# Layer b of a hybrid block on one NeuronCore: its block loop written as one sequence, four engines held to it

## The chip, the cores and the metric

The kernel runs on one NeuronCore of a Trainium2 chip. The metric is the time of one execution on the device, in microseconds (us); the time before is the median of three runs. TensorE (PE) multiplies matrices and PEld is its weight loading; VectorE is DVE, ScalarE is ACT, GpSimd is POOL, SyncE is SP.

## The reference

The input `x` has shape (4, 2048, 512). Four residual steps follow each other, each on a layer-normalised copy of `x`:

```python
x = x + _L0_attn_a_ref(_layernorm(x), ...)   # linear attention, 16 heads of 64
x = x + _L0_ffn_ref(_layernorm(x), L0_ffn_rhs)
x = x + _L0_attn_b_ref(_layernorm(x), ...)   # gated recurrence, below
x = x + _L0_ffn_ref(_layernorm(x), L0_ffn_rhs)
```

The feed-forward step quantises each row to 127 levels, multiplies by a quantised 512 x 512 matrix and scales back. Layer b is the third step with the fourth:

```python
q, k, v = x @ q_w.T, x @ k_w.T, x @ v_w.T            # 16 heads of 32
q, k = _apply_rope(q, cos, sin), _apply_rope(k, cos, sin)
q_r, k_r = einsum('bthd,hrd->bthr', q, Wq), einsum(..., k, Wk)   # 16 features a head
g = sigmoid(x @ g_w.T + g_b)
def step(M, inp):
    q_t, k_t, v_t, g_t = inp
    M = M * decay + einsum('bhr,bhd->bhrd', g_t * k_t * scale, v_t)
    return M, einsum('bhr,bhrd->bhd', q_t, M)
out = Y @ out_w.T + out_b
hres = x + out
return layernorm(hres) * ln_g + ln_b
```

## The kernel before, in words

A flag computed from the decays selects the mild variant of both layers; with these inputs it is the one that runs. `layer_a_mild` does the first two steps and stores its rows to `mmid` in DRAM. `layer_b_mild` does the last two. Only the latter is touched.

Layer b walks 32 blocks of 256 rows (4 sequences of 8 blocks). One turn `n` of the loop works on four blocks at once. `B` is block n: the recurrence itself. `after` is block n+1: its projections. `later` is block n+2: its rows are normalised and turned. `before` is block n-1: its second half of the output projection, and its feed-forward step.

The turn has four chunks, c = 0 to 3, for half a block's rows (`i` = c // 2, a row tile of 128) and a group of 8 heads (`g` = c % 2). In each chunk the recurrence is done in matrix form:

- `scores`: TensorE multiplies keys and queries into `ps`, and the carried `state_b` with the queries into `pyT`; VectorE multiplies `ps` by the causal mask into `ab` (two instructions).
- `update`: TensorE makes `pub` from the turned keys `kt` and the values `vb`; VectorE adds it to `pairs`.
- `outputs`: TensorE adds `ab` times `vb` to `pyT` in two halves; ScalarE copies `pyT` to `yT`; GpSimd spreads `pairs` into `state_b`.

Between these stand the projections. `features` multiplies the turned rows `xnTb` by `m_qT` or `m_kT` into `pr` (8 matmuls of the program, 16 passes in the trace, since float32 matmuls appear as two) and VectorE makes the rotary products `xc`, `xs` out of it. `gates` makes `pg`, from which ScalarE makes `gate`; `keys` makes `pl`, from which ScalarE copies `q` and VectorE makes `k`; `values` makes `pvb`, which ScalarE copies to `vb`. `prepare` weighs keys and queries by powers of the decay: `k1` and `qs` on VectorE, four head-masked query copies on ScalarE, `ke` and `q0` on GpSimd. The keys `ke` are turned by a DMA transpose.

The rows: `enter_row` normalises a row tile into `xr` and starts its turning; `turn_row` ends it. Turning means that VectorE splits the float32 words into 16-bit `planes`, SP issues a DMA transpose to `turned`, and ScalarE joins the halves (`turn_halves`, `join_halves`). `turn_row` also adds `ln_b` and `out_b` on GpSimd. `leave` projects `yT` into `py`, adds `xr` into `h`, normalises it, and adds it to `x` on GpSimd. `finish` is the feed-forward step: `ffn_levels` normalises into `f_xn` and rounds into `f_q`, a DMA transpose makes `f_qT`, TensorE makes `pf`, VectorE scales it into `f_y`, GpSimd adds that to `x`.

Every normalisation is a chain over two engines: `bn_stats` and `bn_aggr` on VectorE, two small operations on GpSimd for `rs` (`stats`, lines 124 to 127), then the scaling on VectorE (`normalize`, line 131).

PSUM is in tagged banks: three for `mm` (all projections), two for `s` (`ps`), two for `y` (`pyT`), one for `u` (`pub`). The pools are single or double buffered, so each tag hands its buffers round in the order in which they are asked for.

What sets the order: the text of the loop gives each chunk a list of small steps (`fill`), which `spread` deals out among the chunk's own steps in equal portions. After that a scheduler of the tile layer may move instructions among each other on every engine. On the chip each engine takes its instructions in the order that results.

```python
def spread(work, fill):
    at = 0
    for n, f in enumerate(work):
        f()
        upto = len(fill) * (n + 1) // len(work)
        for g in fill[at:upto]:
            g()
        at = upto
```

Of the kernel before, what the change touches and what calls it, by code (L numbers as in the profile page):

```python
# [46 lines left out]
def hybrid_block_kernel(ctx: ExitStack, tc: tile.TileContext, t: dict, out: bass.AP):  # L47
# [82 lines left out]
    def normalize(dst, src, mv, rs, i):  # L130
        nc.vector.tensor_scalar(
            dst, src, mv[:, i, 0:1], rs[:, i : i + 1], ALU.subtract, ALU.mult
        )
# [502 lines left out]
    def run(steps):  # L636
        for f in steps:
            f()
# [76 lines left out]
    def join_halves(dst, turned):  # L715

        nc.scalar.copy(  # L717
            dst.bitcast(U16).rearrange("p n (t two) -> p n t two", two=2),
            turned.rearrange("p (two n) t -> p n t two", two=2),
        )  # L720
# [350 lines left out]
    def layer_b_mild():  # L1071
        with ExitStack() as es:
# [23 lines left out]
            def row_tiles():  # L1096
                return rowp.tile([P, KC, TB], F32, name="xnTb"), rowp.tile([P, NTB, D], F32, name="xr", bufs=4)
# [72 lines left out]
            def block(n):  # L1170
                B = Block()
                B.n, B.first, B.x = n, at[n][1] == 0, xs.pop(0) if xs else load_x(n)
                B.qk, B.turned, B.prep, B.yT, B.halves = {}, {}, {}, {}, {}
                return B

            def enter_row(B, i):

                if i == 0:
                    blk = at[B.n][1]
                    B.cs = []  # L1180
                    for name in ("cos", "sin2"):
                        c1 = rowp.tile([P, TB], F32, name=f"m_{name}", bufs=3)
                        queue = nc.scalar if B.n < 2 else nc.sync
                        queue.dma_start(c1, t[name][:, blk * TB : (blk + 1) * TB])
                        B.cs.append(c1.unsqueeze(1).to_broadcast([P, 2, TB]))
                    B.xnT, B.xr = first_rows.pop() if first_rows else row_tiles()
                mv, rs = stats(pool, B.x[:, i : i + 1, :], 1)
                normalize(B.xr[:, i, :], B.x[:, i, :], mv, rs, 0)
                if B.n > 1:
                    B.halves[i] = turn_halves(pool, B.xr[:, i, :])  # L1190

            def turn_row(B, i):
                dst = B.xnT[:, :, i * P : (i + 1) * P]
                if B.n > 1:
                    join_halves(dst, B.halves[i])
                else:
                    transpose_rows(bank, dst, B.xr[:, i, :], tag="mm")
                nc.gpsimd.tensor_tensor(B.x[:, i, :], B.x[:, i, :], ln_b, ALU.add)
                nc.gpsimd.tensor_tensor(B.xr[:, i, :], B.xr[:, i, :], out_b, ALU.add)
# [69 lines left out]
            def prepare(B, g):  # L1269


                q, k = B.qk[g]
                A = Block()
                A.k1 = pool.tile([P, NTB, NQ, P], F32, name=f"k1{g}", bufs=1)
                nc.vector.tensor_tensor(
                    A.k1,
                    k.rearrange("p (i s) -> p i s", s=P).unsqueeze(2).to_broadcast([P, NTB, NQ, P]),
                    tk[:, g, :, :].unsqueeze(1).to_broadcast([P, NTB, NQ, P]), ALU.mult,
                )
                qs = pool.tile([P, NTB * NQ, QB], F32, name="qs", bufs=1)  # L1280
                nc.vector.tensor_tensor(
                    qs, q.rearrange("p (j s) -> p j s", s=QB),
                    tq[:, g, :].unsqueeze(1).to_broadcast([P, NTB * NQ, QB]), ALU.mult,
                )
                A.q1 = pool.tile([P, NTB * NQ, 4, QB], F32, name=f"q1{g}", bufs=1)
                for h in range(4):
                    nc.scalar.activation(A.q1[:, :, h, :], qs, AF.Copy, scale=small["head4"][:, h : h + 1])
                A.ke = pool.tile([P, NTB, P], F32, name="ke", bufs=1)
                A.q0 = pool.tile([P, NTB, P], F32, name=f"q0{g}", bufs=1)
                for dst, src, tab in ((A.ke, k, down), (A.q0, q, up)):  # L1290
                    nc.gpsimd.tensor_tensor(
                        dst, src.rearrange("p (i s) -> p i s", s=P),
                        tab[:, g, 1 : P + 1].unsqueeze(1).to_broadcast([P, NTB, P]), ALU.mult,
                    )
                A.halves = turn_halves(pool, A.ke.rearrange("p i s -> p (i s)"))
                B.prep[g] = A

            def chunk(B, i, g):

                C = Block()  # L1300
                st = state[:, g, :]

                def turn():
                    A = B.prep[g]
                    if i == 0:
                        A.kt = pool.tile([P, NTB, P], F32, name=f"kt{g}", bufs=1)
                        join_halves(A.kt, A.halves)

                def scores():

# [57 lines left out]
                        small["diag"].rearrange("p (q c) -> p q c", c=2 * DB), ALU.mult,  # L1368
                    )

                return [turn, scores, lambda: None, lambda: run([update, outputs]), lambda: None]

            def leave(B, i):

                def evict(py):
                    h = pool.tile([P, D], F32, name="h")
                    nc.vector.tensor_tensor(h, py, B.xr[:, i, :], ALU.add)
                    mv, rs = stats(pool, h.unsqueeze(1), 1)
                    normalize(h, h, mv, rs, 0)
                    nc.gpsimd.tensor_tensor(h, h, ln_g, ALU.mult)  # L1380
                    x = B.x[:, i, :]
                    nc.gpsimd.tensor_tensor(x, x, h, ALU.add)  # L1382

                return product(
                    bank, "py", [P, D],
                    [(lambda c=c: B.yT[i][:, c, :], lambda c=c: wo[:, c, :]) for c in range(KC)], evict,
                )

            def finish(B, i):
                mul = ffn_product(pool, bank, B.x[:, i, :], *ffn_levels(pool, B.x[:, i, :]))  # L1390

                def store():
                    b, blk = at[B.n]
                    nc.sync.dma_start(rows(out[b], blk * TB, TB), B.x)

                return mul + ([store] if i == NTB - 1 else [])

# [7 lines left out]

            for n in range(2):
                for i in range(NTB):
                    enter_row(get(n), i)  # L1410
                    turn_row(get(n), i)
            get(2)
            fill_tables()
# [1 line left out]
            for g in range(G):  # L1415
                run(features(first, "q", g) + features(first, "k", g) + gates(first, g) + keys(first, g))
                run(values(first, g))
                prepare(first, g)
            for n in range(len(at) + 1):
                B, after, later = blocks.get(n), blocks.get(n + 1), blocks.get(n + 2)  # L1420
                before = blocks.get(n - 1)
                if B and B.first:
                    nc.gpsimd.memset(state, 0.0)
                    nc.gpsimd.memset(pairs, 0.0)
                for c in range(2 * G):
                    i, g = c // G, c % G
                    head, fill = [], []
                    if after:
                        fill += [
                            lambda: features(after, "q", 0) + features(after, "k", 0),  # L1430
                            lambda: gates(after, 0) + keys(after, 0) + features(after, "q", 1),
                            lambda: values(after, 0) + features(after, "k", 1),
                            lambda: gates(after, 1) + keys(after, 1) + values(after, 1),
                        ][c]()

                    if c == 0 and before:
                        fill += leave(before, 1)
                        before.mul = finish(before, 0)
                    if c == 1 and before:
                        head = before.mul  # L1440
                    if c == 2 and before:
                        before.mul = finish(before, 1)
                    if c == 2 and B:
                        fill += leave(B, 0)
                    if c == 3 and before:
                        head = before.mul
                    if later and c in (1, 2):
                        head = head + [lambda i=c - 1: turn_row(later, i)]
                    if later and c in (0, 1):
                        enter_row(later, c)  # L1450
                    if c == 2:
                        get(n + 3)
                    work = chunk(B, i, g) if B else [lambda: None]
                    spread(work, head + fill)
                    if c == 2 and after:
                        prepare(after, 0)
                    if c == 3 and after:
                        prepare(after, 1)

    flag = mild_decays()  # L1460
    with tc.If(flag) as mild:
# [111 lines left out]
```

## Time and profile before

| | us |
|---|---|
| median of 3 runs (lowest, highest) | 4069.87 (4067.77, 4070.08) |
| the profiled execution: time, span | 4071.76, 4070.0 |
| TensorE busy (share of the span) | 3922.4 (96%) |
| VectorE busy | 2350.3 (58%) |
| GpSimd busy | 1479.3 (36%) |
| ScalarE busy | 888.8 (22%) |
| mean granted TensorE clock | 0.991 |
| first `ps` of layer b's loop | at 2507.36 |
| last turns' drain (after 4014), until the last GpSimd add ends | 50 |

The span runs from the first to the last instruction; the time has a little around it. Layer a takes about the first 2450 us of the span, layer b the rest. Busy times of TensorE are modelled, and an engine that is busy may also be held back by another; a row's mean can hold both undisturbed and stretched instances of the same operation. In a timeline row the columns are the start, the duration, the engine, the line and operation, the tiles, the count, and in brackets the idle time before it with what ended it. In a wait row they are who waited for whom: us in total, times, longest. In a row for a stretch of time they are the stretch, its length, then busy us and count for TensorE, its weight loads, VectorE, ScalarE and GpSimd, the granted clock, the DMA share and GB/s.

### The profile page before, as it was taken

The page shows a single profiled execution, that of the slowest core. Times are in us where ns is not written, and L with a number is a line of the kernel's source. Part 1 is how long each engine was busy: PE and PEld are TensorE (multiplying, and loading weights), DVE is VectorE, ACT ScalarE, POOL GpSimd, SP SyncE. Part 2 cuts the span into 40 slices and gives each one's busy share as a digit, 9 for nine tenths or more (in the row PEclk, how much of TensorE's full clock was granted, in tenths as well). Part 3 has the DMA queues.
Part 4 walks back from the last instruction along what each step waited for, and adds up shares of the span by engine and source line. Part 5 has one row for each costly group of instructions (what it writes and reads, how often), then busy time and mean ns, then how long its engine had stood idle before and what let it go on. Part 6 is the DMA issues. An engine that isn't in the chain of part 4 may idle for free.

```text
span 4070.0 us, 53718 instructions
## 1 busy us (share of the span) xinstructions
PE 3922.4 (96%) x20821; PEld 2125.6 (52%) x20821; DVE 2350.3 (58%) x4556; ACT 888.8 (22%) x1548; POOL 1479.3 (36%) x2527
## 2 busy tenths in 40 slices
PE   8999999999999999999999987999999999999997
PEld 4554554554555555555555544555555555555553
DVE  4455555555555555555555454666666666666665
ACT  1222122221221222222122111222222222222221
POOL 3223323323333323323332223444444444444443
PEclk9999999999999999999999998999999999999998
DMA  4112212212212222221221123121211112211211
GB/s 135 31 41 55 67 36 60 62 38 64 55 41 65 55 53 52 55 64 40 54 66 39 38 63 111 43 51 48 52 47 47 47 47 50 50 48 49 53 32 29
DMA packets 432042, 217.27 MB, mean 53 GB/s; under 512 B 363808, under 2 KB 376992, under 8 KB 431776
## 3 DMA queue, kind: packets, MB, share of 16 engines
q1 hardware_dynamic: 430656, 212.16, 21.2%
q8 instruction: 166, 2.72, 0.3%
q10 hardware_dynamic: 1120, 1.57, 0.1%
q14 instruction: 100, 0.82, 0.1%
HBM read 91.49 MB, written 34.08 MB: 31 GB/s over the span
## 4 chain that ended last, share of the span: by engine, by line
PE 68%; DVE 18%; POOL 10%; issue 2%; DMA 2%; ACT 0%; SPq 0%; POOLq 0%; ACTq 0%; DVEq 0%
PE pk L648 11%; PE pq L648 11%; PE pv L648 11%; PE po L648 10%; PE py L648 5%; PE pr L1223 4%; PE pss L888 3%; PE pn L974 3%; DVE st L124 3%; POOL rs L127 3%; PE pn L968 3%; DVE planes L710 2%; POOL h L1380 2%; POOL xb L1382 2%; PE pu L904 2%
## 5 line engine op out<-in xcount | busy, mean ns | idle before, releaser
L648 PE MATMUL pq<-xnTa,a_Wq 128*128 128x512 f32 x1024 | 492.2, 608 | 0.0
L648 PE MATMUL pk<-xnTa,a_Wk 128*128 128x512 f32 x1024 | 491.0, 604 | 0.0
L648 PE MATMUL pv<-a_Wv,xnTa 128*128 128x512 f32 x1024 | 476.1, 603 | 2.9 <-ACT xnTa L141 2.9
L648 PE MATMUL po<-a_Wo_sb,oT 128*128 128x512 f32 x1024 | 467.1, 601 | 6.7 <-DVE oT L950 6.7
L126 POOL TENSOR_SCALAR rs<-mv 128x1 f32<-128x1 f32 x320 | 71.7, 224 | 767.6 <-DVE mv L125 767.3
L914 POOL TENSOR_TENSOR within<-state,u 64x64 f32<-64x64 f32 x256 | 157.3, 615 | 524.4 <-ACT u L909 514.8
L648 PEld LDWEIGHTS po<-a_Wo_sb,oT 128*128 128x128 f32 x1024 | 189.6, 190 | 234.9 <-issue 222.1
L648 PEld LDWEIGHTS pv<-a_Wv,xnTa 128*128 128x128 f32 x1024 | 188.6, 191 | 234.2 <-issue 225.2
L648 PEld LDWEIGHTS pq<-xnTa,a_Wq 128*128 128x128 f32 x1024 | 181.4, 189 | 193.1 <-issue 182.8
L648 PEld LDWEIGHTS pk<-xnTa,a_Wk 128*128 128x128 f32 x1024 | 184.5, 189 | 180.9 <-issue 158.8
L909 ACT COPY u<-pu 128x256 f32<-128x256 f32 x128 | 47.7, 373 | 1026.3 <-PE pu L904 1015.4
L1223 PE MATMUL pr<-xnTb,m_qT_sb 128*128 128x256 f32 x1024 | 252.2, 390 | 0.0
L1223 PE MATMUL pr<-xnTb,m_kT_sb 128*128 128x256 f32 x1024 | 248.9, 386 | 0.0
L648 PE MATMUL pvb<-b_vT_sb,xnTb 128*128 128x512 f32 x512 | 242.8, 607 | 0.0
L894 DVE TENSOR_TENSOR sm<-pss,causal 128x512 f32<-128x512 f32 x256 | 164.2, 683 | 119.9 <-PE pss L888 119.9
L648 PE MATMUL py<-b_oT_sb,yT 128*128 128x512 f32 x512 | 231.8, 595 | 0.0
L717 ACT COPY kr<-turned 128x1024 uint16<-128x1024 uint16 x120 | 139.3, 1161 | 423.6 <-DMA turned<-planes 423.6
L1223 PEld LDWEIGHTS pr<-xnTb,m_qT_sb 128*128 128x128 f32 x1024 | 187.6, 190 | 57.3 <-issue 21.4
L1223 PEld LDWEIGHTS pr<-xnTb,m_kT_sb 128*128 128x128 f32 x1024 | 189.9, 190 | 48.9 <-issue 20.0
L127 POOL TENSOR_TENSOR rs<-rs,neg_half 128x1 f32<-128x1 f32 x320 | 193.9, 607 | 23.9
L838 DVE TENSOR_TENSOR xa<-po,xa 128x512 f32<-128x512 f32 x64 | 44.1, 689 | 262.6 <-PE po L648 262.6
L914 POOL TENSOR_TENSOR within<-within,u 64x64 f32<-64x64 f32 x512 | 173.6, 339 | 38.4
(158 smaller groups left out, 6300.0 us busy)
## 6 DMA issues: line engine op xcount, KB each, us to landing
wide<-rec SPq DMA_DIRECT2D x124, 256.0 KB, 3.6
mmid<-xa SPq DMA_DIRECT2D x16, 1024.0 KB, 4.3
out<-xb SPq DMA_DIRECT2D x32, 512.0 KB, 2.8
xa<-in_x SPq DMA_DIRECT2D x15, 1024.0 KB, 6.3
xb<-mmid SPq DMA_DIRECT2D x30, 512.0 KB, 3.6
turned<-planes SPq DMA_TRANSPOSE x304, 3.1
m_cos<-in_cos SPq DMA_DIRECT2D x30, 128.0 KB, 2.3
m_sin<-in_sin SPq DMA_DIRECT2D x30, 128.0 KB, 2.4
```

The lines of the kernel that those rows point to most:

```text
L124: nc.vector.bn_stats(st[:, i, :], x[:, i, :])
L127: nc.gpsimd.tensor_tensor(rs, rs, neg_half[:, :n], ALU.pow)
L648: nc.tensor.matmul(held[0], lhs(), rhs(), start=(n == 0), stop=(n == len(pairs) - 1))
L710: nc.vector.tensor_copy(planes, src.bitcast(U16).rearrange("p (n two) -> p two n", two=2))
L717: nc.scalar.copy(dst.bitcast(U16).rearrange("p n (t two) -> p n t two", two=2), turned.rearrange("p (two n) t -> p n t two", two=2),)
L888: nc.tensor.matmul(ps[h][:, i, :], k[r, chunks[i]], q[r, chunks[i]], start=True, stop=True)
L894: nc.vector.tensor_tensor(s, ps[h], causal.unsqueeze(1).to_broadcast([P, NTA, P]), ALU.mult)
L904: nc.tensor.matmul(pu[r, i, :], A.kr[:, i, r], v()[:, i, vh[h]], start=True, stop=True, skip_group_check=True,)
L914: nc.gpsimd.tensor_tensor(A.before[i + 1][r, r], A.before[i][r, r], u[r, i, :], ALU.add)
L968: nc.tensor.matmul(pn[:, i, :], A.before[i], q[:, chunks[i]], start=(i == 0), stop=False, skip_group_check=True,)
L974: nc.tensor.matmul(pn[r, i, :], v()[:, i, vh[h]], A.sm[h][:, i, :], start=False, stop=True, skip_group_check=True,)
L1223: nc.tensor.matmul(pr[:, half, :], wp[name][:, c, lo : lo + P], B.xnT[:, c, :], start=(c == 0), stop=(c == KC - 1),)
```

## The change

Three things are done, all in `layer_b_mild`.

The helpers are cut where their chain leaves an engine for GpSimd or for a DMA: `enter_row` becomes `weigh_row` (statistics) and `norm_row` (scaling and planes); `leave` becomes `project`, `weigh_output` and `norm_output`; `finish` becomes `weigh_ffn`, `levels` and `store`; the turning of keys becomes `turn_keys` and `turned_keys`.

The loop over chunks with `fill` and `spread` is replaced by one written sequence for a turn, `blocks_of(n)`. In it every chunk begins with `scores`, one or more whole projections follow, then `update` and `outputs`, then the rest.

The loop over turns stands in `tc.manual_schedule` for TensorE, VectorE, ScalarE and GpSimd: these keep the order of the text. SP, which issues the DMAs, is not in the list. The prologue and layer a are outside it.

```diff
-            for n in range(len(at) + 1):
+            def blocks_of(n):
                 B, after, later = blocks.get(n), blocks.get(n + 1), blocks.get(n + 2)
                 before = blocks.get(n - 1)
...
-                for c in range(2 * G):
...
-                    work = chunk(B, i, g) if B else [lambda: None]
-                    spread(work, head + fill)
+                chunks[0][0]()
+                if before:
+                    weigh_ffn(before, 0)
+                if after:
+                    run(features(after, "q", 0))
+                chunks[0][1]()
+                if later:
+                    weigh_row(later, 0)
+                if before:
+                    levels(before, 0)
+                if after:
+                    run(features(after, "k", 0))
+                if before:
+                    project(before, 1)
+                if B:
+                    turned_keys(B, 1)
+                chunks[1][0]()
+                if before:
+                    weigh_output(before, 1)
+                if after:
+                    run(gates(after, 0) + keys(after, 0))
+                chunks[1][1]()
+                if before:
+                    run(before.levels[0])
+                if later:
+                    norm_row(later, 0)
+                if before:
+                    norm_output(before, 1)
+                if later:
+                    weigh_row(later, 1)
+                if after:
+                    run(features(after, "q", 1))
+                chunks[2][0]()
+                if after:
+                    prepare(after, 0)
+                if before:
+                    weigh_ffn(before, 1)
+                if later:
+                    turn_row(later, 0)
+                if after:
+                    run(values(after, 0))
+                    turn_keys(after, 0)
+                chunks[2][1]()
+                if later:
+                    norm_row(later, 1)
+                if before:
+                    levels(before, 1)
+                if after:
+                    run(features(after, "k", 1))
+                if B:
+                    project(B, 0)
+                get(n + 3)
+                chunks[3][0]()
+                if B:
+                    weigh_output(B, 0)
+                if after:
+                    run(gates(after, 1) + keys(after, 1))
+                chunks[3][1]()
+                if before:
+                    run(before.levels[1])
+                    store(before)
+                if after:
+                    prepare(after, 1)
+                if later:
+                    turn_row(later, 1)
+                if B:
+                    norm_output(B, 0)
+                if after:
+                    turn_keys(after, 1)
+                    run(values(after, 1))
+
+            E = mybir.EngineType
+            with tc.manual_schedule(engines={E.PE, E.DVE, E.Activation, E.Pool}):
+                for n in range(len(at) + 1):
+                    blocks_of(n)
```

`scores` (`chunks[c][0]`) and `update` with `outputs` (`chunks[c][1]`) are unchanged inside, and so are `features`, `gates`, `keys`, `values` and, but for the turning of the keys, `prepare`.

## The prediction

> **What bounds the kernel now.** I read the page first, then the waits of TensorE inside layer b's loop, then the loop's timeline.
>
> ```profile
> PE 3922.4 (96%) x20821; PEld 2125.6 (52%) x20821; DVE 2350.3 (58%) x4556; ACT 888.8 (22%) x1548; POOL 1479.3 (36%) x2527
> ...
> PE 68%; DVE 18%; POOL 10%; issue 2%; DMA 2%; ACT 0%; SPq 0%; POOLq 0%; ACTq 0%; DVEq 0%
> ...
> PE pyT L1357 <- DVE ab L1330: 57.4, 116, 1.6
> PE pl L1256 <- issue: 3.8, 1, 3.8
> ...
> 3200.21:3249.10 48.89, 46.95 (x281) 28.11 (x280) 32.43 (x63) 11.53 (x26) 23.29 (x30) 1.00 0.20 49
> ```
>
> TensorE is busy 96% of the span. The two wait rows cover 2480 to 4010 us, which is all of layer b's steady part: TensorE waits for one thing only, VectorE's masked scores `ab`. The last line is one loop turn: TensorE 46.95 of 48.89 us, VectorE 32.43, ScalarE 11.53, GpSimd 23.29, clock 1.00. The starts of the first score product `ps` repeat every 48.9 us over turns 2 to 29. So a turn is TensorE's work plus what it waits for `ab`. Why does `ab` come late?
>
> ```profile
> 3211.64 1.13 PE L1317 MATMUL ps<-q,k 64*128 64x512 f32 x4
> 3212.60 0.39 PE L1324 MATMUL pyT<-q,state_b 64*128 64x128 f32 x4
> 3212.92 1.98 PE L648 MATMUL pvb<-b_vT_sb,xnTb 128*128 128x512 f32 x4
> 3214.74 2.32 PE L1223 MATMUL pr<-xnTb,m_kT_sb 128*128 128x256 f32 x10
> 3216.99 0.32 PE L1344 MATMUL pub<-vb,kt 128*32 128x64 f32 x8
> 3218.08 0.43 PE L1357 MATMUL pyT<-ab,vb 128*32 128x128 f32 x8 [0.77 <-DVE ab L1330]
> 3218.68 0.42 PE L1357 MATMUL pyT<-ab,vb 128*32 128x128 f32 x8 [0.17 <-DVE ab L1330]
> 3219.03 1.56 PE L1223 MATMUL pr<-xnTb,m_kT_sb 128*128 128x256 f32 x6
> ...
> 3215.10 0.67 DVE L668 TENSOR_SCALAR f_xn<-f_xn,f_sc 128x512 f32<-128x512 f32 x1
> 3215.81 0.43 DVE L670 TENSOR_SCALAR f_q<-f_xn 128x512 bf16<-128x512 f32 x1
> 3216.15 0.68 DVE L1231 TENSOR_TENSOR xc_q<-pr,m_cos 128x512 f32<-128x512 f32 x1
> 3217.35 1.28 DVE L1330 TENSOR_TENSOR ab<-ps,m_causal 128x512 f32<-128x512 f32 x2
> ```
>
> The scores are done at 3212.77. Until 3217.35 VectorE works off feed-forward levels and rotary products that stand ahead of `ab`; then TensorE, stopped, waits. From `pub` to the resumed `pr` takes 2.04 us here (3216.99 to 3219.03); where nothing waits it takes 0.14 + 0.55 = 0.69. Lost: 1.35. The same spot in chunk 0 loses 1.40. Together 2.75 of each turn, more than the idle column's 1.93[...]. Work without waits: 48.89 - 2.75 = 46.14 us a turn.
>
> **The change part by part.** No arithmetic is added or removed. In the built order each chunk opens with `ps`, its state product and, on VectorE, `ab` at once; then comes one whole projection, then `pub` and the output products.
>
> *Whole chains.* Before, a turn has 7 interruptions of a projection (`pr` as 4+12, 10+6, 8+8; `pvb` as 4+4; `pg` as 2+6; one output product in halves). Start to start, 16 `pr` passes take 3.45 us whole (2491.83 to 2495.28); the same 16 cut cost about 0.1 more per cut (8 before `ps` take 1.82, not 1.73). Gain: 7 x 0.1 = 0.7 us a turn. Checked by adding segments, start to start: `ps` 0.96, state product 0.32, `pub` 0.14, outputs 0.55 per chunk (1.97 x 4 = 7.88); four `pr` at 3.53, 0.08 more than from `pr` to `pr` since another kind of product follows (14.12); two `pvb` at 3.55 (7.10); two `py` at 3.52 (7.04); two `pg` at 1.92 (3.84); two `pl` at 1.87 (3.74); two `pf` at 0.86 (1.72). Sum 45.44.
>
> *The late `ab`.* With `ab` first, it needs VectorE free when `ps` ends, or at most 2.5 us later: between lie 0.32 + about 3.55 + 0.14, less 1.28 for `ab`. I walk VectorE through a turn in the new order. Chunk 0 carries about 8.7 us of VectorE work in 12.5 us of TensorE time, chunk 1 about 9 in 10.1, chunk 2 about 10 in 12.6, chunk 3 about 7 in 10.1. In the tightest place, chunk 1 into 2, the rotary product `xc_q` waits for its `pr` until chunk 1 + 10.3, and `ab` of chunk 2 ends near chunk 2 + 4.0 against a need at 5.0. Chunk 2 into 3 is as tight. So all four `ab` come in time: 2.75 us a turn removed.
>
> *What is late next.* Two new places.
> First, `bn_stats` of chunk 0 stands on VectorE ahead of `xc_q`, `pairs` and the levels, and waits for GpSimd's `xb`+`h`. In chunk 3 GpSimd now runs the feed-forward add `xb`+`f_y` (from about 7.6 us into the chunk), `ke`, `q0`, `ln_b`, `out_b`, `ln_g`, `xb`+`h`: 1.27 + 0.73 + 0.72 + 1.28 + 1.27 + 1.28 + 1.27 = 7.8, done at 15.4, that is about 5.3 into the next chunk 0. VectorE stands still for about 3 us there, catches up by chunk 0 + 13, and `ab` of chunk 1 is in time. Cost nothing; the cover is the 3.6 us of room in chunk 0.
> Second, and this I charge: the next turn's first `pr` reads both rows of `xnTb`. ScalarE, which keeps its order, copies the second row only after the four head-masked queries of chunk 3. Into chunk 3: `pf` starts at 5.75 and ends at 6.78, `f_y` 7.53, then `k1`, `qs`, four masked queries 1.71, the copy 1.16, hand-overs 0.2. The `pr` wants it at 10.13 + 1.28 = 11.41.
>
> Here the mean rows (`k1` 0.644, `qs` 0.589) give 7.53 + 1.23 + 3.07 = 11.83, a wait of 0.4. But these rows are mixtures: both take 0.41 alone, and an operation that meets GpSimd is stretched:
>
> ```profile
> 3208.09 1.27 POOL L1198 TENSOR_TENSOR xb<-xb,b_ln_b_row 128x512 f32<-128x512 f32 x1 [0.66 <-DVE xr L131]
> 3208.53 1.38 DVE L710 COPY planes<-xr 128x1024 uint16<-128x1024 uint16 x1
> ```
>
> The copy (0.68 at best elsewhere) ends 0.55 after GpSimd's add has ended at 3209.36. The Trainium skill, "SBUF — State Buffer", section "SBUF: two separate sides", calls the port pair that VectorE and GpSimd share an exclusive lock, held for the whole instruction, so the loser blocks. It speaks against this change, since in chunk 3 GpSimd's row of adds starts exactly when `k1` and `qs` do. By that rule `k1` goes first (0.41), the add follows (1.27), `qs` after it (0.41 to 0.6): `qs` ends at 9.6 and `xnTb` at 12.6, a wait of 1.15. Lower end 0 (alone: 0.82 for both, 11.42); upper end 1.6 (the add first, then `ke` between). I take 1.15, nearest to the rows above.
>
> *DMAs.* SP is not among the held engines. Per turn it issues the same ten transfers; the transpose of the next rows' planes moves later by a chunk, the transpose of `ke` moves ahead of the row load. A transpose lands about 2.6 us after its planes (f_q end 4033.91, `pf` 4036.46). Every consumer is at least 3 us further off: `f_qT` is issued before chunks 1 and 3 begin and read 5.75 us into them; `kt` of group 1 is issued after the store, 11 us into chunk 3, and read in chunk 1. Cost nothing; an issue takes 1.2 us, so three queued would use up that cover.
>
> *Start and end.* Turns 0 and 1 take 92.3 us before (2505.97 to 2598.29). After: 45.44 less `py` 3.5 and two `pf` is 40.2 for turn 0, 45.44 for turn 1, and 1.15 twice, so 87.9: gain 4.4. Turn 30 has nothing later to wait for: 46.2 against 45.4, gain 0.8. The drain (50 us before, from 4013.9) is a chain of normalise, transpose, product, GpSimd add; walked in the new order it comes to 51: loss 1.
>
> *Sum.* A turn: 45.44 + 1.15 = 46.6 against 48.9, gain 2.3; 28 such turns, 64.4. With 4.4 + 0.8 - 1 it is 68.6. The profiled execution took 4071.8 us (span 4070.0), 1.9 over the median of the runs, 4069.87. So 4069.9 - 68.6 = 4001.
>
> **The rivals.**
> *No new wait.* `k1` and `qs` slip in ahead of GpSimd's adds: 45.44 a turn, 28 x 3.46 + 6 = 103, giving 3967. For it: some `k1` do take 0.41. Against: GpSimd is loaded in just that stretch.
> *The wait only moves.* VectorE's 32 us are stretched by the lock until `ab` is again about as late as now (or `pr` as late by the same 2.7). Only the whole chains are gained, 30 x 0.7 = 21: 4049. For it: 1 us of room in two of four places. Against: chunk 0 has plenty, and `ab` is now first in line.
> *Slower, by the port.* The place is `qs` in chunk 3. If GpSimd keeps the pair through its unbroken row `xb`+`f_y`, `ke`, `q0`, `ln_b`, `out_b`, `qs` ends not at 9.6 but near 14.2, ScalarE's copy at 17.2, and TensorE stops for 5.7 us a turn: 51.1 against 48.9, so 28 x 2.2 = 62 more, 4132. It decides from a wait of 3.46 us, when `qs` ends after 11.8. Against it: where VectorE meets back-to-back GpSimd adds in this trace, it gets in after one (the longest stretched rows are 1.5 us).
> *It does not do what it says:* the built order does follow the text on all four engines, so I give this nothing.
>
> **How the numbers follow.** The forecast 4001 (wait of 0.4 to 1.6) has 0.58; no wait, 0.17; the wait only moves, 0.14; slower by the port, 0.09; about no change, 0.02. The likeliest gives 4001. The range 3967 to 4042 reaches the no-wait case and most of the moved-wait case. A difference of 0.2%, 8 us, is about what a measurement can tell from no change. Faster 0.89, same 0.02, slower 0.09.
>
> **What would show it right or wrong.** Right: the wait of `pyT` for `ab`, 57.4 us, all but gone; `pr` in runs of 16; `ps` of chunk 0 every 46.6 us; a new TensorE wait of about 1.1 us a turn at `pr` with `m_qT` for ScalarE's `xnTb`; VectorE idle before `st` of `xb`, waiting for GpSimd. Wrong: waits of `pyT` for `ab` still above 1 us a turn, a turn above 47.5 us, or `pf` waiting for its transpose inside the loop.

## The result, and the profile after

The kernel after takes 4024.81 us (median of four runs, 4023.89 to 4026.71) against 4069.97 for the kernel before (four runs, 4067.77 to 4070.50). The ratio is 0.9891, with a 95% interval of 0.9874 to 0.9908: 45 us faster. The forecast was 4001, in a range of 3967 to 4042. In the profiled executions the span goes from 4070.0 to 4023.4, that is 46.6 less, where 68.6 had been summed up. Two things are therefore to be explained: where 46.6 came from, and where 22 of the expected 68.6 went.

The page of the kernel after, its busy times and its chain that ended last:

```profile
PE 3896.8 (97%) x20821; PEld 2133.2 (53%) x20821; DVE 2401.1 (60%) x4556; ACT 877.8 (22%) x1548; POOL 1516.3 (38%) x2527
...
PE 90%; DVE 3%; ACT 2%; POOL 2%; DMA 2%; issue 1%; SPq 0%; ACTq 0%; POOLq 0%; DVEq 0%
```

The chain is now nearly all TensorE's: VectorE's share of it fell from 18% to 3%, GpSimd's from 10% to 2%. The instruction counts are those of before, as they must be when only order changes. The waits of TensorE over 2480 to 3980 us, layer b's steady part, say what it still stops for:

```profile
PE pr L1230 <- ACT xnTb L717: 18.7, 26, 0.7
PE pyT L1333 <- POOL state_b L1442: 15.1, 3, 5.0
...
PE pyT L1366 <- DVE ab L1339: 1.5, 4, 0.8
```

The wait for `ab`, 57.4 us before, is gone but for 1.5, all of it behind 3960, where the last turns begin; the steady turns have none. The first row is the forecast's new wait, 0.72 us once in a turn. The second row was in nobody's sum: three waits of 5 us for a GpSimd memset (L1442).

An ordinary turn starts its first `ps` every 46.53 us (2592.50, 2639.03, 2685.56 and so on), against 46.6 in the forecast and 48.9 before. Its first chunk in the timeline of the kernel after:

```profile
3204.71 0.39 PE L1333 MATMUL pyT<-q,state_b 64*128 64x128 f32 x4
3205.82 3.72 PE L1230 MATMUL pr<-xnTb,m_qT_sb 128*128 128x256 f32 x16 [0.72 <-ACT xnTb L717]
3209.47 0.32 PE L1353 MATMUL pub<-vb,kt 128*32 128x64 f32 x8
3209.60 0.62 PE L1366 MATMUL pyT<-ab,vb 128*32 128x128 f32 x16
```

`pr` comes as 16 passes in one piece, and the 16 passes of `pyT` with `ab` come as one group: neither half waits. The wait has moved to the head of `pr`, with ScalarE's copy named as its end. What made that copy late is in chunk 3 of the turn (start, duration, engine, what was done):

```profile
3246.95 0.75 DVE L683 SCALAR_TENSOR_TENSOR f_y<-pf,f_sc,rscale 128x512 f32<-128x512 f32 x1 [0.57 <-PE pf L681]
3247.62 0.41 DVE L1282 TENSOR_TENSOR k<-k,tk 128x256 f32<-128x256 f32 x1
3247.78 1.38 POOL L684 TENSOR_TENSOR xb<-xb,f_y 128x512 f32<-128x512 f32 x1 [0.59 <-DVE f_y L683]
3247.95 1.49 DVE L1288 TENSOR_TENSOR qs<-q,tq 128x256 f32<-128x256 f32 x1
3249.54 1.71 ACT L1294 ACTIVATE q<-qs,m_head 128x256 f32<-128x256 f32 x4 [3.26 <-DVE qs L1288]
3251.15 1.15 ACT L717 COPY xnTb<-turned 128x1024 uint16<-128x1024 uint16 x1
```

`k1` (its output tile is `k`) runs in 0.41 just ahead of GpSimd's add. `qs`, the same kind and size of operation, takes 1.49: it starts 0.17 after the add and ends at 3249.44, 0.28 after the add has ended at 3249.16. ScalarE's four masked queries and then its copy of `xnTb` follow one behind the other.

The turn shown above is followed by one that begins a new sequence (n = 24). There the timeline of the kernel after reads:

```profile
3254.65 1.26 POOL L1397 TENSOR_TENSOR xb<-xb,h 128x512 f32<-128x512 f32 x1
3255.85 0.53 POOL L1442 MEMSET state_b<- 128x512 f32 x1
...
3256.43 0.80 PE L1333 MATMUL pyT<-q,state_b 64*128 64x128 f32 x4 [5.02 <-POOL state_b L1442]
3257.16 5.37 PE L1230 MATMUL pr<-xnTb,m_qT_sb 128*128 128x256 f32 x16
```

The memset that clears the carried state stands at the head of the turn's text. GpSimd, now held to the text, reaches it only after the last of its adds from chunk 3, and TensorE's state product waits 5.02 us. After the wait, `pr` takes 5.37 instead of 3.72. The row for the stretch around it (the granted clock is the first number behind GpSimd's count) goes with that:

```profile
3254.00:3260.00 6.00, 3.57 (x11) 2.81 (x12) 0.88 (x2) 0.00 (x0) 3.23 (x6) 0.50 0.21 77
```

The clock is 0.50 there and 1.00 again from 3261 on; a steady turn shows 1.00. It fell about 2.3 us into the wait (1.00 up to 3253.6, 0.50 from 3253.8). Three such turns (n = 8, 16, 24) take 52.9, 53.0 and 53.1 us. In the kernel before, the scheduler had put this memset right behind chunk 3's last `state_b`, 3.6 us ahead of the first `ps` of the new sequence and ahead of the two adds of `turn_row`:

```profile
2889.18 0.73 POOL L1365 TENSOR_TENSOR state_b<-pairs,m_diag 128x256 f32<-128x256 f32 x1
2889.96 0.53 POOL L1423 MEMSET state_b<- 128x512 f32 x1
...
2893.56 1.27 POOL L1198 TENSOR_TENSOR xb<-xb,b_ln_b_row 128x512 f32<-128x512 f32 x1 [0.36 <-DVE xr L131]
```

The drain lost time too. From the first `ps` of turn 31 to the end of the span it took 56.1 us before (from 4013.87) and takes 62.1 after (from 3961.26). The last turn, n = 32, only finishes block 31; three rows of its timeline in the kernel after:

```profile
3999.49 1.89 PE L681 MATMUL pf<-rq,f_qT 128*128 128x512 bf16 x4 [6.78 <-DMA f_qT<-f_q]
4001.42 0.75 DVE L683 SCALAR_TENSOR_TENSOR f_y<-pf,f_sc,rscale 128x512 f32<-128x512 f32 x1 [2.91 <-PE pf L681]
4002.09 0.54 DVE L131 TENSOR_SCALAR h<-h,mv,rs 128x512 f32<-128x512 f32 x1
```

The normalisation of `h` (L131) does not need `f_y`; it only stands behind it. Its statistics are done when GpSimd's `rs` ends at 3999.48. In the kernel before the same normalisation ran ahead of its `f_y`:

```profile
4047.86 0.55 DVE L131 TENSOR_SCALAR h<-h,mv,rs 128x512 f32<-128x512 f32 x1 [1.00 <-POOL rs L127]
...
4051.74 0.73 DVE L683 SCALAR_TENSOR_TENSOR f_y<-pf,f_sc,rscale 128x512 f32<-128x512 f32 x1
```

### The profile page after: what moved, and what is told of

It is laid out like the page before. It is cut to its first block, busy times and chain, and to the rows that moved or that the text cites. A ratio compares the mean times of both kernels' runs of the same rounds, so it can differ in the third digit from the quotient of the medians.

```text
span 4023.4 us, 53593 instructions
## 1 busy us (share of the span) xinstructions
PE 3896.8 (97%) x20821; PEld 2133.2 (53%) x20821; DVE 2401.1 (60%) x4556; ACT 877.8 (22%) x1548; POOL 1516.3 (38%) x2527
## 4 chain that ended last, share of the span: by engine, by line
PE 90%; DVE 3%; ACT 2%; POOL 2%; DMA 2%; issue 1%; SPq 0%; ACTq 0%; POOLq 0%; DVEq 0%
PE pr L1230 12%; PE pk L648 11%; PE pv L648 11%; PE pq L648 11%; PE po L648 11%; PE py L1386 5%; PE pss L888 3%; PE pn L974 3%; PE pvb L648 3%; PE pg L648 3%; PE pl L1263 3%; PE pf L681 3%; PE pn L968 3%; PE ps L1326 3%; PE pu L904 2%
## 5 line engine op out<-in xcount | busy, mean ns | idle before, releaser
L126 POOL TENSOR_SCALAR rs<-mv 128x1 f32<-128x1 f32 x320 | 81.9, 256 | 1055.3 <-DVE mv L125 1052.2
L1230 PE MATMUL pr<-xnTb,m_qT_sb 128*128 128x256 f32 x1024 | 240.6, 389 | 18.7 <-ACT xnTb L717 18.7
L1339 DVE TENSOR_TENSOR ab<-ps,m_causal 128x512 f32<-128x512 f32 x256 | 164.5, 684 | 131.6 <-PE ps L1326 131.6
L1230 PE MATMUL pr<-xnTb,m_kT_sb 128*128 128x256 f32 x1024 | 237.9, 385 | 0.0
L648 PE MATMUL pvb<-b_vT_sb,xnTb 128*128 128x512 f32 x512 | 234.6, 601 | 0.0
L1230 PEld LDWEIGHTS pr<-xnTb,m_qT_sb 128*128 128x128 f32 x1024 | 196.1, 194 | 54.4 <-ACT xnTb L717 23.7
L683 DVE SCALAR_TENSOR_TENSOR f_y<-pf,f_sc,rscale 128x512 f32<-128x512 f32 x128 | 96.0, 750 | 198.3 <-PE pf L681 198.1
```

What stands on the lines that cost most here:

```text
L648: nc.tensor.matmul(held[0], lhs(), rhs(), start=(n == 0), stop=(n == len(pairs) - 1))
L1230: nc.tensor.matmul(pr[:, half, :], wp[name][:, c, lo : lo + P], B.xnT[:, c, :], start=(c == 0), stop=(c == KC - 1),)
L1339: nc.vector.tensor_tensor(C.a[:, half, :, :].rearrange("p h (j s) -> p h j s", s=QB), ps[half].rearrange("p j h s -> p h j s"), small["cau ...
```

## The experiments

Each edit is against the kernel after unless it says otherwise. The runs of the kernel before beside them had medians of 4069.3 to 4070.8.

**The memset, put where the state is last read.**

```diff
-                if B and B.first:
+                if B and B.first and n == 0:
                     nc.gpsimd.memset(state, 0.0)
                     nc.gpsimd.memset(pairs, 0.0)
...
                 chunks[3][1]()
+                if B and after and after.first:
+                    nc.gpsimd.memset(state, 0.0)
+                    nc.gpsimd.memset(pairs, 0.0)
```

> The changed kernel with one thing moved: the two GpSimd memsets that zero state_b and pairs at the start of a sequence stand in chunk 3 of the turn before, right after that chunk's state_b, instead of at the head of the turn. Theory A (the memsets, held behind GpSimd's tail of adds, stop TensorE for 5.0 us at three sequence starts, and the idle time lowers the clock so that the next 16 pr passes take 5.4 instead of 3.7): the three long turns of 52.9 us become 46.5, 3 x 6.4 = 19 us less than the changed kernel, near 4005 to 4006. Rival B (the long turns come from the clock or from GpSimd's tail itself, whatever the memsets' place): turns of 52.9 stay, near 4025. Rival C (the wait is partly replaced by another on the same tail): a gain of 5 to 15.

Measured: 4005.27 us (4003.32 to 4005.97), ratio 0.9839 with an interval of 0.9823 to 0.9856; 19.5 below the kernel after. No long turn is left, all from turn 2 on are 46.52 to 46.54, and the row for `state_b` is gone from the waits, while the one for `xnTb` stays. So the place of the memset is the whole of the 3 x 6.4 us, what the lowered clock cost included.

**`qs` ahead of `k1`.** Only the order of these two VectorE operations in `prepare` is exchanged.

> The changed kernel with qs computed before k1 on VectorE in prepare. Theory A (exclusive port: the operation that stands directly behind f_y slips in ahead of GpSimd's add, the next one waits until the add has ended; this stretch of qs is what makes the copy of xnTb late by 0.79 us a turn at the first pr): in chunk 3 qs takes 0.41 and ends about 1.4 us sooner, k1 takes 1.5, the wait of pr for xnTb (18.7 us in total) goes to 0, and a turn takes 45.7 to 45.8; 28 x 0.75 = 21 us less, near 4004. Rival B (the stretch is shared bandwidth, not a lock; or ScalarE's copy waits for its DMA transpose and not for qs): the wait of pr stays at 0.4 to 0.7 a turn, gain under 10 us.

Measured: 4005.32 us (4004.18 to 4007.04), ratio 0.9842 with an interval of 0.9826 to 0.9859. The ordinary turn is 45.74, and TensorE no longer waits for `xnTb`. In this kernel's timeline the two have changed roles:

```profile
3234.95 0.41 DVE L1282 TENSOR_TENSOR qs<-q,tq 128x256 f32<-128x256 f32 x1
3235.11 1.38 POOL L684 TENSOR_TENSOR xb<-xb,f_y 128x512 f32<-128x512 f32 x1 [0.60 <-DVE f_y L683]
3235.28 1.49 DVE L1287 TENSOR_TENSOR k<-k,tk 128x256 f32<-128x256 f32 x1
```

The first one through takes 0.41 and the second 1.49, whichever they are. The duration belongs to the place in the order, not to the operation. Since `k` only feeds GpSimd's `ke`, its delay costs nothing. The long turns at a sequence's start remain, as they should (53.0, 54.1 and 53.0 us). (The diff moves the five lines of `qs` above those of `k1`.)

**The new text without the hold.**

```diff
-            with tc.manual_schedule(engines={E.PE, E.DVE, E.Activation, E.Pool}):
-                for n in range(len(at) + 1):
-                    blocks_of(n)
+            for n in range(len(at) + 1):
+                blocks_of(n)
```

> The changed kernel's written sequence without the holding: the loop over turns stands outside the manual schedule, so the scheduler may move instructions on all engines. Theory A (the written sequence brings the gain of a turn; the holding only fixes the memsets and the tail in bad places): the steady turn stays within 0.5 us of 46.5, the 52.9 us turns vanish since the scheduler puts the memsets back into chunk 3, so about 4003 to 4010, faster than the held one. Rival B (the holding is what keeps ab first; a free scheduler mixes feed-forward levels in front of ab again): waits of pyT for ab return, a turn of 47.5 to 48.9, 4035 to 4068.

Measured: 4332.60 us (4331.91 to 4334.22), ratio 1.0646 with an interval of 1.0628 to 1.0663. Both sizes were missed by far; the rival's mechanism is the right one, but a turn takes 58.0, which is 11.5 over 46.53 where the rival allowed 2.4 at most. One wait row of TensorE (2480 to 4280 us) and two spots in the timeline of this kernel:

```profile
PE pyT L1366 <- DVE ab L1339: 216.3, 92, 4.5
...
2872.63 0.42 PE L1366 MATMUL pyT<-ab,vb 128*32 128x128 f32 x8 [2.90 <-DVE ab L1339]
...
3129.74 0.43 DVE L670 TENSOR_SCALAR f_q<-f_xn 128x512 bf16<-128x512 f32 x1
3130.08 1.28 DVE L1339 TENSOR_TENSOR ab<-ps,m_causal 128x512 f32<-128x512 f32 x2
3130.82 1.25 PE L1366 MATMUL pyT<-ab,vb 128*32 128x128 f32 x16 [4.45 <-DVE ab L1339]
...
3129.50:3135.50 6.00, 4.68 (x24) 3.27 (x25) 3.21 (x7) 1.49 (x3) 0.72 (x1) 0.50 0.63 149
```

TensorE's own order here is that of the text. VectorE's is not: the scheduler put the feed-forward levels before `ab`, which stands first in the text, and TensorE, with whole chains and nothing to slip in, waits 4.45 us. The clock falls to 0.50, as the last row shows; `pyT` takes 1.25 for 0.62 and the next `pr` 5.67 for 3.72. Wait and clock together make 7.0 of the 7.2 us by which this chunk is longer than one without a wait (19.93 against 12.70). After the shorter wait of 2.90 the clock is 0.50 too, from 2873.2 to 2876.5.

**The old text with the hold** (edit against the kernel before: its own loop, unchanged, inside `tc.manual_schedule` for the four engines).

> The kernel before, its own loop with spread, but held on the same four engines. Theory A (holding an order in which bn_stats, the GpSimd rs and the scaling stand directly behind each other makes VectorE stop at every hop to GpSimd, and ab stands behind it): each turn has 6 normalisations with about 1.0 us of GpSimd hop each plus two waits for x at the tail of GpSimd; VectorE's 32 us become 40 to 45, ab comes later than before, a turn of 50 to 56 us: 4100 to 4290. Rival B (holding in itself is what helps, the cutting of the chains does little): a turn of 46 to 48 us, 3990 to 4045.

Measured: 4365.68 us (4364.48 to 4369.09), ratio 1.0729 with an interval of 1.0711 to 1.0747. The direction is that of theory A, the size above its range. A turn is 58.7 us on average; TensorE waits 233.5 us for `ab` in the loop, up to 4.6 at a time, and the mean clock over 2500 to 4300 us is 0.94. The mechanism of theory A is at most a part of it: VectorE's stops for `rs` add up to 7.6 us a turn here and to 6.8 in the kernel before, while it now also stands 4.2 us a turn for ScalarE's `q` and 4.0 for `pr`. Which of these makes `ab` late was not taken apart. So each half of the change alone costs 260 to 300 us, and only both together gain 45. The gain is not the sum of two effects.

**Only VectorE held.**

```diff
-            with tc.manual_schedule(engines={E.PE, E.DVE, E.Activation, E.Pool}):
+            with tc.manual_schedule(engines={E.DVE}):
```

> The changed kernel with only VectorE held to the written order; TensorE, ScalarE and GpSimd are left to the scheduler, which on GpSimd puts the memsets into chunk 3 of the turn before. Theory A (what the holding does is keep VectorE's ab ahead of the feed-forward levels, as the not-held run with 58 us turns suggests): turns of 46 to 47 us, no turn above 48, 4000 to 4010. Rival B (another engine's order, GpSimd's above all, matters as much, for VectorE waits for rs from it): waits for ab return, a turn above 48, over 4065.

Measured: 3981.96 us (3979.68 to 3984.01), ratio 0.9784 with an interval of 0.9769 to 0.9799. The turn is 45.74 and no turn is long. The scheduler did by itself what the first two edits did by hand, the second in another way. It put the memset into chunk 3, and ScalarE's copy of the second row tile into the end of chunk 2, ten us ahead of the masked queries of chunk 3:

```profile
3183.46 1.49 DVE L1288 TENSOR_TENSOR qs<-q,tq 128x256 f32<-128x256 f32 x1
...
3219.78 1.16 ACT L717 COPY xnTb<-turned 128x1024 uint16<-128x1024 uint16 x1 [1.28 <-DMA turned<-planes]
...
3229.04 0.52 POOL L1442 MEMSET state_b<- 128x512 f32 x1
```

In an ordinary turn `qs` still takes 1.49 (first row), but no copy stands behind it, and it costs nothing. Beside the run without any hold, this puts a value on each part: VectorE's order is worth 351 us (4332.60 to 3981.96), and holding the other three costs 43 (4024.81 to 3981.96). How the 43 divide among TensorE, ScalarE and GpSimd was not tried one by one; the rows above show a share of GpSimd and one of ScalarE.

**Two projections cut again.** The first `pr` is cut 8+8 around chunk 0's `update` and `outputs`, one `pvb` 4+4 around chunk 2's.

```diff
-                    run(features(after, "q", 0))
+                    work = features(after, "q", 0)
+                    run(work[:4])
                 chunks[0][1]()
+                if after:
+                    run(work[4:])
...
```

> The changed kernel with two projections of a turn cut in halves again: pr for the queries in chunk 0 as 8+8 passes and pvb in chunk 2 as 4+4, each with update and outputs in the gap; everything else as it was. Theory A (an interruption costs TensorE about 0.1 us, as the sum of the prediction has it): a turn of 46.7 to 46.8 instead of 46.53, 6 us more in all, and no new wait for ab, since about 1 us of room is left. Rival B (an interruption costs nothing by itself, only the wait for ab did): 46.5. Rival C (with half of the cover gone, ab is late): waits of pyT for ab of 0.3 to 1 us a turn.

Measured, in one run: 4023.42 us, and a turn of 46.53 to the hundredth as without the cuts. Rival B holds: a cut is free. The timeline of this kernel around the second cut and the first:

```profile
3182.91 1.98 PE L648 MATMUL pvb<-b_vT_sb,xnTb 128*128 128x512 f32 x4
3184.73 3.62 PE L1230 MATMUL pr<-xnTb,m_kT_sb 128*128 128x256 f32 x16
...
3205.88 0.32 PE L1353 MATMUL pub<-vb,kt 128*32 128x64 f32 x8
...
3206.56 1.99 PE L1230 MATMUL pr<-xnTb,m_qT_sb 128*128 128x256 f32 x8
3208.39 3.62 PE L1230 MATMUL pr<-xnTb,m_kT_sb 128*128 128x256 f32 x16
```

The second half now runs straight into the next `pr`, so the pause of about 0.1 us has only changed its place: a `pr` that stands straight behind `pyT` takes 3.56 from its start to that of the next product (3163.62 to 3167.18 in the kernel after), and here it takes 3.46 (3208.39 to 3211.85), while the half behind `pyT` takes 1.83 (3206.56 to 3208.39) where half of 3.46 is 1.73. It takes 3.45 behind the half of `pvb`, which is another kind of product (3184.73 to 3188.18). So the pause is not paid between two projections, whose rows all say 128*128, but where TensorE goes from a projection to the small products of the recurrence (64*128, 128*32) and back. A cut costs only if it adds such a passage, and these two add none.

**The last turn's normalisation ahead of `f_y`.**

```diff
                 chunks[1][1]()
+                if before and not B:
+                    norm_output(before, 1)
                 if before:
                     run(before.levels[0])
                 if later:
                     norm_row(later, 0)
-                if before:
+                if before and B:
                     norm_output(before, 1)
```

> The changed kernel with one exchange in the last turn, in which only the finished block is left: norm_output of its row tile 1 stands ahead of the feed-forward product of its row tile 0. Theory A (in the drain, VectorE's scaling of h stands behind f_y, which waits 2.9 us for the product and its DMA transpose; GpSimd's ln_g and its add follow only then): the last GpSimd add ends 3 to 4 us sooner after the last ps, the span is 3 to 4 us shorter. Rival B (the drain is long because of the lower clock and the serial transposes): under 1 us.

Measured, in one run: 4022.52 us. That alone is within what a measurement can tell from no change, so the trace is read: from turn 31's first `ps` (3961.26 after, 3961.95 here) to the end of the last GpSimd add (4017.44, 4014.69) it is 56.2 us after and 52.7 here, 3.4 less, as theory A had it. Before it was 50.0 (4013.87 to 4063.88). What the other 2.7 went into was not tried; the mean clock over these stretches is 0.82 before, 0.76 after and 0.78 here, so rival B's clock may have a share.

**The three edits together** (memset, `qs` first, last turn).

> The changed kernel with the memsets moved into chunk 3 of the turn before, qs ahead of k1, and the exchange in the last turn. If the three causes are separate, their gains add: about 65.5 for the memsets' kernel against the kernel before, 22 more for the shorter turn (28 x 0.79) and 3 for the drain: 3979 to 3984. If two of them share a wait, one gain is lost: 3990 or more.

Measured: 3978.51 us (3974.79 to 3981.98, five runs), ratio 0.9776 with an interval of 0.9763 to 0.9789. The edits more than add up: 19.5, 19.5 and 3.4 taken off 4024.81 give 3982.4, and it was 3.9 less, with a turn of 45.74 throughout. The traces account for about 3.6 of these: turns 2 to 29 take 41.4 us less than after, where the two edits alone gave 19.3 and 18.6. With `qs` first alone the three long turns gained nothing (160.1 us together, against 158.9 after), since the wait for the memset covers the one for `xnTb` there; with the memset moved they gain as any other turn.

**One `ab` made late again.** In the kernel of the three edits, the mask of chunk 2 is put behind `prepare`, `weigh_ffn` and the planes of the keys on VectorE; TensorE's text is as it was.

```diff
-                return scores, lambda: run([update, outputs])
+                return scores, lambda: run([update, outputs]), mask
...
                     turn_keys(after, 0)
+                chunks[2][2]()
                 chunks[2][1]()
```

> The combined kernel with one thing put back: in chunk 2 VectorE does qs, k1, bn_stats and the planes of ke before ab instead of after it; no other order changes. Theory A (the late ab is what a turn of the kernel before lost: there an idle time of 0.77 + 0.17 us cost 1.35 us[...]): ab of chunk 2 ends its first half about 5.9 us into the chunk against a need at 5.04, so pyT waits 0.8 to 1.0 us and then 0.17, and the turn is 1.2 to 1.5 us longer than 45.74, 46.9 to 47.2. Rival B (TensorE's waits for ab were only a symptom, the turn was held by something else, such as the interrupted chains): a turn of 45.7 to 46.1 although pyT waits.

Measured, in one run: 4020.68 us; a turn is 46.96 (3195.13, 3242.09, 3289.06), 1.23 more than 45.74. The two halves in the timeline of this kernel:

```profile
3234.06 0.43 PE L1373 MATMUL pyT<-ab,vb 128*32 128x128 f32 x8 [0.64 <-DVE ab L1346]
...
3234.65 0.42 PE L1373 MATMUL pyT<-ab,vb 128*32 128x128 f32 x8 [0.17 <-DVE ab L1346]
```

Shown as idle are 0.64 + 0.17 = 0.81; lost are 1.23. This is the same pair of rows as in the kernel before (0.77 and 0.17, reckoned there at 1.35), made anew by nothing but VectorE's order. It shows that the late `ab` costs about one and a half times its idle column; a part of the difference is that the two halves take 0.43 and 0.42, where the product in one piece takes 0.62. Rival B, by which the turn would have stayed at 45.7 to 46.1, is refuted.

**Only VectorE held, and the last turn's exchange.**

> The kernel in which only VectorE is held, with the exchange in the last turn on top (norm_output of row tile 1 ahead of the feed-forward product of row tile 0). The turn stays at 45.74 by every theory. Theory A (the drain's loss is VectorE's order alone, so it is there too): 2 to 4 us less than with VectorE held alone, 3978 to 3980. Rival B (with GpSimd free the drain was already repaired): no difference, 3981 to 3983.

Measured: 3978.15 us (3975.08 to 3978.78), ratio 0.9775 with an interval of 0.9759 to 0.9791. The median is 3.8 under that of VectorE held alone, but the intervals overlap, so the times do not tell the two apart. The trace does: from turn 31's first `ps` (3915.09 here, 3917.66 there) to the end of the last GpSimd add (3967.22, 3973.17) it is 52.1 us here and 55.5 there. This and the kernel of the three edits come out alike, 2.2% under the kernel before and 1.2% under the kernel after.

## Why the prediction was right, and where it was not

The sign and the mechanism were right, and the turn too, though by two errors that cancel; the sum was 22 us too large, mainly for one omitted term and one that was mis-sized. Against the forecast's terms, in us of the profiled spans:

| term | forecast | measured | from |
|---|---|---|---|
| 28 turns | 64.4 (2.3 each) | 66.5 (2.37 each) | 48.91 to 46.53 |
| turns 0 and 1 | 4.4 | 5.8 | turn 2 begins at 2598.29 (its `ps` at 2600.11, with 1.82 of `pr` drawn ahead of it) and at 2592.50; neither turn waited for `xnTb`, for which the forecast had charged 1.15 twice |
| three sequence starts | not there | -19.3 | 53.0 on average against 46.53, three times |
| turn 30 | 0.8 | -0.3 | 46.2 to 46.54 |
| turns 31 and 32 | -1 | -6.0 | 56.1 to 62.1 |
| sum | 68.6 | 46.7 | spans: 46.6 |

*The late `ab`: right.* The -2.75 a turn was the largest term. The rows for `ab` went from 57.4 us to 1.5, and the late `ab` put back in one chunk cost 1.23, where the forecast had reckoned 1.35 for such a spot.

*Whole chains: too large, and wrong in reason.* The forecast took 0.1 for each of 7 cuts, 0.70 a turn. The timeline of before shows six projections cut; the seventh, an output product in halves, is the late `ab` itself. Its work of a turn was 45.44; with no wait left it was measured at 45.74, which makes the gain 48.91 - 2.75 - 45.74 = 0.42. And the two cuts put back cost nothing: what is paid is the passage between projections and the small products. Counted in the timelines, a turn before has nine runs of projections between small products and a turn after has eight; at twice 0.1 for a run, an estimate from the rows above, that is 0.2 of the 0.42, and the rest is not attributed. The step "about 0.1 more per cut" is the one that failed, by 0.28 a turn. The check by segments failed with it: it put all four `pr` at 3.53, where they take 3.55, 3.56, 3.56 and, between small products on both sides, 3.65.

*The new wait: right in kind, too large by 0.36.* The forecast took 1.15 between bounds of 0 and 1.6, by the lock rule of the Trainium skill, "SBUF — State Buffer", section "SBUF: two separate sides", and the row of the stretched copy. Measured: 0.72 idle, 0.79 of a turn (46.53 against 45.74 without it). The order of events is that of the rule: `k1` 0.41, GpSimd's add, `qs` 0.28 after the add's end, at 9.33 us into the chunk against 9.6. The mean rows had given 0.4. Exchanging `k1` and `qs` took the wait away and left the rest of the turn as it was, so the meeting with GpSimd's add is shown as its cause. That a lock on a port lies behind it is the page's account: the rows agree with it, and no run tests it against another. The two errors, -0.28 and +0.36, cancel; that the turn came out within 0.1 is luck. (Three small sums of the forecast are off and decide nothing: 12.6 less 11.41 is 1.2 and not 1.15, the room ahead of `ab` adds up to 2.7 and not 2.5, and the row of five GpSimd operations would end `qs` near 13.7 and not 14.2.)

*The rivals.* "No new wait" was refuted by the 0.72, "the wait only moves" by the rows for `ab`, 1.5 us in all and none in the steady turns. In "slower, by the port", GpSimd's unbroken row kept `qs` out until 14.2; VectorE got in after one add. The stretch of 3 us in which VectorE stands before `st` is there (3.22 before the long turn, 3.24 in an ordinary one, at 3209.43), and no TensorE wait for `ab` follows it, as said.

*The start of a sequence: the step that was missing.* The walk of GpSimd in chunk 3 went up to its last add, "done at 15.4, that is about 5.3 into the next chunk 0", and found that VectorE can afford it. The memset at the head of the turn's text was not in the walk, since it is there in only three steady turns. From that same 5.3 the wait could have been read: TensorE's state product wants `state_b` 0.96 into the chunk, and it came some 5 us late. Of the 6.4 us, about 4.3 are wait (5.02, less the 0.72 that it covers) and the rest is the clock at 0.50: 1.65 in `pr` and 0.4 in the state product. The Trainium skill, "TensorE: Matmul & The Clock Gate", section "HAM oscillation — how this bites in real kernels", warns of TensorE gaps above about 3.4 us. The trace agrees that such gaps lower the clock: with waits of 5.02 and 4.45 it was 0.50 for about 7 us, with waits of 0.7 it stayed at 1.00. It does not bear the figure out as a limit: the wait of 2.90 in the kernel without the hold was followed by 0.50 as well, and of two waits in the old text with the hold, the one of 2.12 us (at 2750.91) was followed by 0.50 and the one of 2.13 (at 2867.91) by 1.00. So no sharp limit shows here.

*The drain: mis-sized.* The walk gave 51 for 50. The held order put one normalisation behind an `f_y` that comes late only in the last turn, where no other work fills the transposes. That accounts for 3.4 of the 6.0, by the exchange; the rest stays open. Turn 30 took 46.5 as any other where 45.4 was forecast for want of a later turn. There the forecast had misplaced its own wait: the first `pr` of turn 30 reads the rows that ScalarE copied in turn 29, and it waits for them as in every turn (0.72, before the `pr` at 3916.80). That is 0.79 of the 1.1; the other 0.3 is the turn's work, 45.74 and not 45.44.

*What made the change work* was not asked in the forecast. The hold of VectorE to the new text did: it keeps `ab` at the front. That whole chains without it are the worse for being whole, because TensorE has nothing else in line when `ab` is late, fits the row of the 4.45 us wait, but no run shows it by itself.

## What to carry to other kernels

Hold the engine whose order feeds the bound engine, and leave the others to the scheduler until a trace shows that it does worse: here VectorE's hold alone gave 88 us, and holding three more gave 43 of it back. When an order is written by hand, walk the rare instructions as well as the steady turn (what is reset between sequences, what is last), since a scheduler will have moved them without a word. And of two operations of which the second meets a GpSimd add and is held up by it, put the one that someone waits for first.

## What the runs showed of the hardware

- TensorE waits of 4.45 and 5.02 us went with a granted clock of 0.50 for about 7 us, which began while TensorE still waited; a wait of 2.90 was followed by 0.50 for about 3.3. The 5.02 us of waiting cost 6.4.
- The pause between matmul groups, about 0.1 us, goes with the passage between projections (128*128) and the small products of the recurrence (64*128, 128*32). Behind `pyT` a `pr` takes 3.56, behind `pvb` or another `pr` 3.45 to 3.46, and two cuts left the turn at 46.53.
- A wait that breaks a product in two costs more than its idle column: 0.81 us of idle, before two halves, cost 1.23. The wait of 0.72 ahead of a whole `pr` cost 0.79.
- A VectorE operation that starts 0.16 us ahead of GpSimd's add takes 0.41; the same kind of operation that starts 0.17 behind it takes 1.49.
